# Local attention: queries and keys projected two groups ahead, transposed behind the half-array run; row 0's weights turned in blocks of 32 on VectorE

## The chip, the cores and the metric

The kernel runs on one core of one Trainium2 chip, in 32-bit floating point throughout. A core has five engines with a queue of their own each, which work in order and wait for one another through semaphores: TensorE (PE in the profile; its weight loads are shown apart as PEld), VectorE (DVE), ScalarE (ACT), GpSimd (POOL) and SyncE (SP), which here issues all DMAs. TensorE writes into eight banks of PSUM, from which VectorE and ScalarE copy ("evict") the results to SBUF. The metric is the time on the device in microseconds.

## What is computed

The input x has 2 sequences of 4096 tokens with 256 channels. A first layer (RWKV style) adds a recurrence over time to x. Then come two identical layers, each with local attention and a gated feed-forward part. Cut to what the change touches, one such layer is:

```python
h = shift_token(x)                       # half of the channels one token later
q, k, v = split(h @ wqkv, 3)             # 8 heads of 64
q = l2norm(q) * q_scale ; k = l2norm(k) * k_scale
q, k = rotary_xpos(q, k)                 # q*cos*scale + rotate_half(q)*sin*scale
# windows of 128 tokens: each query sees itself and the 128 tokens before it
attn = softmax(where(mask, -big, q @ k.T), -1)
x = x + (attn @ v) @ wo
h = layernorm(shift_token(x)) ; a, g = split(h @ w1 + b1, 2)
x = x + (a * gelu(g)) @ w2 + b2
```

The mask leaves a query at place i of its window the places above or at i of the window before (packs and backs in the kernel are the two triangles) and the places up to i of its own.

## The kernel before

**Groups and rows.** The attention layers run over 128 groups of 128 tokens (NN = 128; a block is four groups, and there are 32 blocks: 2 sequences x 2 layers x 8). The loop `for n in range(NN + 2)` (L1469) goes over the groups; its pass n is called row n here. In row n stand, among others, the scores, softmax and transposed weights of group n, the values and the output of group n - 1, q, k and v of group n + 1, and pieces of the feed-forward part of earlier blocks (fill). The recurrence of the second sequence is spread over some 50 rows of the first; the recurrence of the first sequence comes before the loop.

**Who sets the order.** The statements do not run in the order written. `Plan.note` records every operation with the row it belongs to (`plan.at`), its dependencies, and a cost from `Plan.cost` (L302). `Plan.order` (L376) then plays the engines forward: each time the engine that can start soonest takes, of the operations that can start at that time, the one of the lowest row and place. It knows how the eight banks come free, the shared lock of VectorE and GpSimd, the landing of DMAs, and a cost `TURN` when TensorE changes between its full array and a half of it. Operations marked `either` go to ScalarE or VectorE as they come free. `give` emits the result, so each engine's queue is fixed when the kernel is built, and every instruction has one line, L524 (L520 and L518 for scalings).

**The half-array run.** In `scores` (L1086) TensorE multiplies keys and queries of 64 rows each (`row` half), two heads side by side; in the same uninterrupted piece, `down_ends` comes ahead in some rows and `values(n - 1)` (L1183) follows, whose matmuls have 64 columns (`col` half): weights of the own window (pT with v) and of the window before (pB with dv, the difference of neighbouring v, made by GpSimd from a shifted copy vr). So one stretch per row runs on half arrays, and is entered from and left to full matmuls.

**q and k.** `project(n, j)` (L989) makes q (j = 0), k (1) or v (2) of group n: two matmuls of 128x512 into a bank, and a copy. `square` (ScalarE), `norms` (VectorE sum, then a power on GpSimd for the inverse root), `rotate` (GpSimd), `cosines` and `rotated` (VectorE) make the normalised, rotated q and k in place in `qk` (two buffers). `transpose_qk(n)` (L1062) turns them by eight TensorE transposes through two banks into qT and into one of three places of kT; on every second group a DMA copies one place of kT to another. It stands at the top of row n, ahead of the scores of group n.

**Row 0 of pB.** `transpose_p(n, s)` (L1157) turns the softmax weights of four heads at a time; ScalarE or VectorE copies them to pT, and VectorE multiplies them by the mask backs into pB. Row 0 of pB is different: it is the first column of pr, the weight of the oldest place. At s = 1 a ninth transpose, of 128x8, turns that column for all eight heads; a copy takes its 8 rows from PSUM to `last`, and one DMA writes them into row 0 of pB. The matmuls of values(n) that read pB wait for that DMA.

Of the kernel before, what the change touches and what calls it, by code (L numbers as in the profile page):

```python
# [15 lines left out]
P = 128  # L16
B, S, D = 2, 4096, 256
HD_A = 16
L, HEADS, DH, W = 2, 8, 64, 128
# [42 lines left out]
SLACK = 1.06  # L62
LOAD = 1283
LAND = 2500
TURN = {"row": 195, "col": 95, "full": 199}
SETS = {AF.Exp: 1, AF.Tanh: 1, AF.Gelu: 2, AF.Ln: 3}
QUADS = 4

# [112 lines left out]
class Plan:  # L181
# [194 lines left out]
    def order(self):  # L376
# [49 lines left out]
        while todo:  # L426
            for e in engines:
                if e not in stale:
                    continue
                best = None  # L430
                cands = []
                for t, g in waiting[e]:
                    s = earliest(e, t, g)
                    if e == "vector" and g[0].eng == "either" and free["scalar"] < max(t, free[e]) + LEAN:
                        continue
                    if s is not None:
                        cands.append((max(s, free[e]), g))
                if not cands:
                    pick[e] = None
                    continue  # L440
                t0 = min(s for s, _ in cands)
                for s, g in cands:
                    if s <= t0 + 1:
                        key = g[0].at
                        if best is None or key < best[0]:
                            best = (key, s, g)
                pick[e] = (best[1], best[2])
            stale = set()
            e = min((e for e in engines if pick[e]), key=lambda e: pick[e][0], default=None)
            assert e is not None, "no operation can start"  # L450
            t, g = pick[e]
            for o in g:
                if e == "tensor" and o.half != half:
                    t += TURN[o.half]
                    half = o.half
                if e == "scalar" and o.set not in (None, table):
                    t += LOAD
                    table = o.set
                for p in o.banks:
                    b = min((i for i in range(8) if banks[i] is not None), key=lambda i: banks[i])  # L460
                    p.bank, banks[b] = b, None
                    p.real = self.bank_tiles[b]
                    counts[p] = (len(p.users), 0.0)
                step, time = o.step, o.time
                if o.eng == "either" and e == "vector":
                    n = o.outs[0].idx.size
                    time = 150 + 1.04 * n if o.name == "copy" else 155 + 0.98 * n
                    step = time - 85
                    o.lock, o.hold = o.name == "scaled", time
                if o.eng == "either":  # L470
                    o.eng = e
                if e not in ("tensor", "sync"):
                    step, time = step * SLACK, time * SLACK
                o.start = t
                if e == "sync":
                    dma = max(dma, t) + o.passes
                    o.end = max(t + time, dma + LAND)
                else:
                    o.end = t + time
                if o.lock and e in lock:  # L480
                    lock[e] = t + o.hold
                t += step
                done.append(o)
                for p in o.uses:
                    c, last = counts[p]
                    counts[p] = (c - 1, max(last, o.end))
                    if c == 1:
                        banks[p.bank] = counts[p][1]
                        stale.add("tensor")
            free[e] = t  # L490
            if g[0].lock:
                stale.update(lock)
            stale.update(("vector", "scalar") if e == "scalar" else (e,))
            for x in engines:
                n = len(waiting[x])
                waiting[x] = [c for c in waiting[x] if c[1] is not g]
                if len(waiting[x]) != n:
                    stale.add(x)
            for nxt in after.get(id(g), ()):
                left[id(nxt)] -= 1  # L500
                if not left[id(nxt)]:
                    ready(nxt)
                    stale.update(("scalar", "vector") if nxt[0].eng == "either" else (nxt[0].eng,))
            todo -= 1
# [23 lines left out]
def kernel(ctx: ExitStack, tc: tile.TileContext, a: dict, out: bass.AP):  # L528
# [329 lines left out]
    w2 = tile_of([P, NM, D], "w2")  # L858

    def weights(l, which):  # L860
        if "qkv" in which:
            for j in range(3):
                cols = slice(j * INNER, (j + 1) * INNER)
                nc.sync.dma_start(out=wqkv[:, :, cols], in_=a["w_qkv"][l][:, :, cols])
        if "o" in which:
# [244 lines left out]
    def softmax(n, g):  # L1110
# [42 lines left out]
        for m in range(2):  # L1153
            ph = prs[n][:, h0 + 2 * m, off:]
            nc.either.scaled(ph, ph, sums[:, m : m + 1])

    def transpose_p(n, s):  # L1157


# [14 lines left out]
            ALU.mult,  # L1174
        )
        if s:
            pt = bank([P, W])
            nc.tensor.transpose(pt[:HEADS, :], pr[:, :, 0], ident)
            last = tile_of([P, W], "last", 2)[:HEADS]
            either(last, pt[:HEADS, :])  # L1180
            nc.sync.dma_start(out=pBs[n][0:1], in_=last)

    def values(n):  # L1183

# [268 lines left out]
    rec2.start()  # L1453
    plan.at(-1)
    nc.gpsimd.memset(ends, 1.0)
    load(0)
    mixed_out(0)
    transpose_x(0)
    load(1)
    table(0)  # L1460
    for j in range(3):
        project(0, j)
    square(0)
    rotate(0, 0)
    rotate(0, 1)
    norms(0)
    cosines(0)
    rotated(0)
    for n in range(NN + 2):  # L1469
        k, w = divmod(n, NW)  # L1470
        here, ahead, behind = n < NN, n + 1 < NN, 0 < n <= NN
        plan.at(n)
        if here:
            transpose_qk(n)
        for c in range(rec2.n):
            if NW + 1 + int(c * R_SLOTS / rec2.n) == n:
                plan.at(n + 0.5)
# [7 lines left out]
        plan.at(n)  # L1485

        first, l = ahead and (n + 1) % (NB * NW) == 0, ((n + 1) // (NB * NW)) % L
        if w == 3 and k + 2 < NK:
            load(k + 2)
        if w == 0 and k + 1 < NK:  # L1490
            mixed_out(k + 1)
        if 1 < n < NN + 2:
            normed(hs[(n - 2) // NW][:, (n - 2) % NW, :])
        if ahead:
            table(n + 1)
            if first:
                weights(l, "qkv")
            project(n + 1, 0)
            rotate(n + 1, 0)
        if here:  # L1500
            scores(n)
            differences(n)
        else:
            with piece():
                if n == NN:
# [4 lines left out]
        if here:  # L1510
            softmax(n, 0)
            softmax(n, 1)
        if ahead:
            project(n + 1, 1)
            square(n + 1)
            rotate(n + 1, 1)
        if behind:
            output(n - 1)
            shift(n - 1)
# [1 line left out]
                weights(n // (NB * NW) % L, "o")  # L1521
        if w == 1 and 0 < k < NK:
            transpose_h(k - 1)
        if w == 2 and k + 1 < NK:
            transpose_x(k + 1)
        if here:
            softmax(n, 2)
            softmax(n, 3)
        if ahead:
            norms(n + 1)  # L1530
        fill(n, 0)
        if here:
            transpose_p(n, 0)
        if ahead:
            project(n + 1, 2)
            cosines(n + 1)
        fill(n, 1)
        if here:
            transpose_p(n, 1)
        if ahead:  # L1540
            rotated(n + 1)
        fill(n, 2)
        fill(n, 3)
        if w < 2 and NW < n < NN and (n - NW - w) % (NB * NW) == 0:
# [83 lines left out]
```

## Time and profile before

| | |
|---|---|
| median of 3 runs | 2966.02 us (2964.07 to 2966.45) |
| the profiled execution | 2965.18 us, its span from first to last instruction 2963.4 us |
| TensorE busy | 2942.4 us, 99% of the span |
| VectorE, ScalarE, GpSimd busy | 76%, 68%, 49% |
| granted TensorE clock | 1.0 in all slices |
| transposes of row 0 on TensorE | 124 |
| copies to last | 97 on ScalarE, 250 ns; 27 on VectorE, 269 ns (medians) |
| DMAs pB<-last | 124, 693 ns each on SyncE's queue (median) |

A group of the profile is named by the tiles it writes and reads: `bank<-mats,pr` are transposes of softmax weights (mats holds the identity), `bank<-mats,qk` those of q and k, `bank<-wqkv,xT` the projections, `bank<-kT,qT` the scores, `bank<-pT,vt` and `bank<-pB,dv` the values, `bank<-hT,w` and `bank<-w,hm` the feed-forward part, `bank<-wo,oT` the output. `128*64` after it are the rows and columns of the array that are used. A 32-bit matmul is recorded as two instructions, a transpose as one. Matmuls overlap in the array, so the durations of a group add up to more than the time it takes; the distance between starts tells that time.

### The profile page before, as it was taken

How to read it: one execution, taken by the hardware profiler on the slowest of the kernel's cores; microseconds unless marked ns; L12 is line 12 of the kernel's file. 1: busy time of each engine (PE TensorE's matmuls, PEld its weight loads, DVE VectorE, ACT ScalarE, POOL GpSimd, SP SyncE). 2: the span in 40 equal slices, each digit the busy share in tenths (PEclk: the TensorE clock that was granted, in tenths of full speed). 3: DMA queues.
4: the chain of work that ended last, by engine and by line, in shares of the span. 5: the costliest groups of instructions: out<-in, count | busy, mean ns of one | idle time of the engine just before them, and what ended most of it. 6: DMA issues, size and time to landing. Idle time of an engine off the chain costs nothing.

```text
span 2963.4 us, 49081 instructions
## 1 busy us (share of the span) xinstructions
PE 2942.4 (99%) x15592; PEld 1919.1 (65%) x15592; DVE 2253.5 (76%) x5095; ACT 2023.8 (68%) x5377; POOL 1449.2 (49%) x1705
## 2 busy tenths in 40 slices
PE   9999999999999999999999999999999999999999
PEld 4476766666666666666666666666666666666667
DVE  7889999998866788786777667777776676767674
ACT  7887787778666777776666666665666666666664
POOL 2226654555554555445555444444554554555550
PEclk9999999999999999999999999999999999999999
DMA  2324322221121211111122221121112211111110
GB/s 85 114 78 135 113 69 88 74 81 54 60 65 54 79 49 54 59 57 56 54 71 84 75 66 50 58 62 58 58 41 71 70 58 51 56 53 54 49 42 28
DMA packets 185228, 195.10 MB, mean 66 GB/s; under 512 B 27812, under 2 KB 148484, under 8 KB 184456
## 3 DMA queue, kind: packets, MB, share of 16 engines
q1 hardware_dynamic: 184968, 191.96, 21.1%
q8 instruction: 123, 2.02, 0.3%
q14 instruction: 137, 1.12, 0.1%
HBM read 85.46 MB, written 39.85 MB: 42 GB/s over the span
## 4 chain that ended last, share of the span: by engine, by line
PE 90%; DVE 5%; ACT 4%; issue 1%; DMA 0%; POOL 0%; ACTq 0%; DVEq 0%; POOLq 0%
PE bank L524 90%; ACT pr L524 1%; ACT L524 1%; DVE arena L524 1%; DVE sq L524 1%; DVE bank L524 1%; ACT pr L520 1%; DVE hm L524 0%; DVE nmx L524 0%; DVE qk L524 0%; DVE x L524 0%; DVE pB L524 0%; DVE rn L524 0%; ACT hm L524 0%; ACT arena L524 0%
## 5 line engine op out<-in xcount | busy, mean ns | idle before, releaser
L524 PE MATMUL bank<-wqkv,xT 128*128 128x512 f32 x1536 | 723.8, 596 | 0.5 <-ACT xT L524 0.5
L524 PE MATMUL bank<-hT,w 128*128 128x512 f32 (+2 forms) x1452 | 651.7, 582 | 0.4 <-ACT hT L524 0.4
L524 POOL TENSOR_TENSOR t<-qk,tab 128x256 f32<-128x256 f32 x512 | 385.0, 772 | 467.9 <-ACT qk L524 360.5
L524 ACT ACTIVATE pr<-bank,nmx 128x129 f32<-128x129 f32 (+1 forms) x1024 | 370.6, 381 | 149.2 <-DVE nmx L524 147.9
L524 PEld LDWEIGHTS bank<-hT,w 128*128 128x128 f32 (+1 forms) x1452 | 262.7, 188 | 252.9 <-issue 237.7
L524 PEld LDWEIGHTS bank<-wqkv,xT 128*128 128x128 f32 x1536 | 266.4, 191 | 210.9 <-issue 207.5
L524 POOL TENSOR_TENSOR rn<-rn,mhalf 128x16 f32<-128x16 f32 x128 | 391.7, 3060 | 8.7
L520 ACT ACTIVATE pr<-pr,sums 128x129 f32<-128x129 f32 (+1 forms) x948 | 334.1, 419 | 40.5 <-DVE pr L524 40.1
L524 DVE COPY_PREDICATED bank<-packs,bank 128x254 f32<-128x254 int32 x496 | 186.4, 420 | 228.5 <-PE bank L524 228.3
L524 PE MATMUL bank<-w,hm 128*128 128x256 f32 x1280 | 294.2, 381 | 0.0
L524 POOL TENSOR_TENSOR dv<-vr,vt 128x512 f32<-128x512 f32 x124 | 164.6, 1327 | 200.2 <-PE bank L524 187.2
L524 PEld LDWEIGHTS bank<-w,hm 128*128 128x128 f32 x1280 | 239.7, 190 | 35.0 <-issue 4.2
L524 ACT COPY qk<-bank 128x512 f32<-128x512 f32 x225 | 132.6, 589 | 170.6 <-PE bank L524 164.1
L524 PE MATMUL bank<-kT,qT 64*128 64x256 f32 (+1 forms) x2048 | 246.1, 380 | 0.4 <-ACT kT L524 0.4
L524 PE MATMUL bank<-wo,oT 128*128 128x256 f32 x1024 | 243.3, 380 | 2.2 <-ACT oT L524 2.0
L524 PEld LDWEIGHTS bank<-wo,oT 128*128 128x128 f32 x1024 | 193.3, 190 | 71.9 <-ACT oT L524 24.2
L524 PEld LDWEIGHTS bank<-kT,qT 64*128 64x128 f32 x2048 | 190.4, 187 | 68.8 <-issue 35.2
L524 DVE TENSOR_TENSOR pB<-bank,backs 128x512 f32<-128x512 f32 x248 | 170.2, 686 | 82.6 <-PE bank L524 56.1
L524 ACT COPY hm<-bank 128x512 f32<-128x512 f32 (+1 forms) x175 | 100.8, 576 | 178.3 <-PE bank L524 177.3
L524 ACT ACTIVATION_READ_ACCUMULATOR pr<-bank,nmx 128x1 f32 x1024 | 222.3, 217 | 0.0
L524 PEld LDWEIGHTS bank<-mats,pr 128*128 128x128 f32 x1148 | 134.5, 135 | 115.9 <-issue 73.0
L524 PE MATMUL bank<-pT,vt 128*64 128x128 f32 x2048 | 203.3, 279 | 0.0
(159 smaller groups left out, 5628.8 us busy)
## 6 DMA issues: line engine op xcount, KB each, us to landing
vr<-vt SPq DMA_DIRECT2D x124, 224.0 KB
tab<-in_c_rot_dram SPq DMA_DIRECT2D x128, 128.0 KB
kT<-kT SPq DMA_DIRECT2D x64, 256.0 KB
z<-zd SPq DMA_DIRECT2D x16, 512.0 KB
x<-in_x_dram SPq DMA_DIRECT2D x16, 512.0 KB
x1d<-x SPq DMA_DIRECT2D x16, 512.0 KB
x<-x1d SPq DMA_DIRECT2D x16, 512.0 KB
h<-x SPq DMA_DIRECT2D x128, 64.0 KB
```

The source lines that it names most:

```text
L520: self.nc.scalar.activation(dst, src, AF.Copy, scale=scale)
L524: getattr(getattr(self.nc, o.eng), name)(*args, **kw)
```

## The change

Four things are changed together.

1. q and k of group n + 2, no longer of n + 1, are projected, normalised and rotated in row n; those of groups 0 and 1 come before the loop. v stays one group ahead. The weights of a new layer are loaded for q and k in the row that first projects with them, those for v one row later; `transpose_x` moves from the third row of a block to the second.
2. `transpose_qk(n + 1)` is noted in row n behind the scores of group n, no longer at the top of its own row. The transposes of group 0 come before the loop.
3. In `Plan.order`, when TensorE stands on a half array, transposes that can start within 150 ns of the earliest candidate are taken ahead of all else, and leaving the half array by a transpose is charged 150 ns (full matmul: 199). The charges for entering the row and the column half are exchanged (95 and 195).
4. Row 0 of pB: the ninth transpose, its bank and its copy go. GpSimd copies the 128x8 column of weights into a square of 128x32 (two buffers, cleared once), VectorE transposes it in blocks of 32x32, and four DMAs write the first eight rows of each block of 32 partitions to row 0 of pB, 32 places each.

```diff
@@ -62,7 +62,7 @@
 SLACK = 1.06
 LOAD = 1283
 LAND = 2500
-TURN = {"row": 195, "col": 95, "full": 199}
+TURN = {"row": 95, "col": 195, "full": 199, "turn": 150}
 SETS = {AF.Exp: 1, AF.Tanh: 1, AF.Gelu: 2, AF.Ln: 3}
 QUADS = 4
 
@@ -439,7 +439,13 @@
                     pick[e] = None
                     continue
                 t0 = min(s for s, _ in cands)
-                for s, g in cands:
+
+                turns = [] if e != "tensor" or half == "full" else [
+                    c for c in cands if c[0] <= t0 + TURN["turn"] and c[1][0].name == "transpose"
+                ]
+                if turns:
+                    t0 = max(s for s, _ in turns)
+                for s, g in turns or cands:
                     if s <= t0 + 1:
                         key = g[0].at
                         if best is None or key < best[0]:
@@ -451,7 +457,7 @@
             t, g = pick[e]
             for o in g:
                 if e == "tensor" and o.half != half:
-                    t += TURN[o.half]
+                    t += TURN["turn" if o.name == "transpose" else o.half]
                     half = o.half
                 if e == "scalar" and o.set not in (None, table):
                     t += LOAD
@@ -858,8 +864,8 @@
     w2 = tile_of([P, NM, D], "w2")
 
     def weights(l, which):
-        if "qkv" in which:
-            for j in range(3):
+        for j, t in enumerate("qkv"):
+            if t in which:
                 cols = slice(j * INNER, (j + 1) * INNER)
                 nc.sync.dma_start(out=wqkv[:, :, cols], in_=a["w_qkv"][l][:, :, cols])
         if "o" in which:
@@ -1154,6 +1160,8 @@
             ph = prs[n][:, h0 + 2 * m, off:]
             nc.either.scaled(ph, ph, sums[:, m : m + 1])
 
+    squares = [tile_of([P, 32], f"square{i}") for i in range(2)]
+
     def transpose_p(n, s):
 
 
@@ -1174,11 +1182,12 @@
             ALU.mult,
         )
         if s:
-            pt = bank([P, W])
-            nc.tensor.transpose(pt[:HEADS, :], pr[:, :, 0], ident)
-            last = tile_of([P, W], "last", 2)[:HEADS]
-            either(last, pt[:HEADS, :])
-            nc.sync.dma_start(out=pBs[n][0:1], in_=last)
+
+            q, t = squares[n % 2], tile_of([P, 32], "turned", 2)
+            nc.gpsimd.tensor_copy(q[:, :HEADS], pr[:, :, 0])
+            nc.vector.transpose(t, q)
+            for i in range(0, W, 32):
+                nc.sync.dma_start(out=pBs[n][0:1, :, i : i + 32], in_=t[i : i + HEADS, :])
 
     def values(n):
 
@@ -1453,25 +1462,33 @@
     rec2.start()
     plan.at(-1)
     nc.gpsimd.memset(ends, 1.0)
+    for t in squares:
+        nc.gpsimd.memset(t, 0.0)
     load(0)
     mixed_out(0)
     transpose_x(0)
     load(1)
     table(0)
-    for j in range(3):
-        project(0, j)
-    square(0)
-    rotate(0, 0)
-    rotate(0, 1)
-    norms(0)
-    cosines(0)
-    rotated(0)
+    project(0, 2)
+    for n in range(2):
+        if n:
+            plan.at(0)
+            table(n)
+        for j in range(2):
+            project(n, j)
+        square(n)
+        rotate(n, 0)
+        rotate(n, 1)
+        norms(n)
+        cosines(n)
+        rotated(n)
+        if n == 0:
+            transpose_qk(0)
     for n in range(NN + 2):
         k, w = divmod(n, NW)
         here, ahead, behind = n < NN, n + 1 < NN, 0 < n <= NN
         plan.at(n)
-        if here:
-            transpose_qk(n)
+        next2 = n + 2 < NN
         for c in range(rec2.n):
             if NW + 1 + int(c * R_SLOTS / rec2.n) == n:
                 plan.at(n + 0.5)
@@ -1485,21 +1502,24 @@
         plan.at(n)
 
         first, l = ahead and (n + 1) % (NB * NW) == 0, ((n + 1) // (NB * NW)) % L
+        first2, l2 = next2 and (n + 2) % (NB * NW) == 0, ((n + 2) // (NB * NW)) % L
         if w == 3 and k + 2 < NK:
             load(k + 2)
         if w == 0 and k + 1 < NK:
             mixed_out(k + 1)
         if 1 < n < NN + 2:
             normed(hs[(n - 2) // NW][:, (n - 2) % NW, :])
-        if ahead:
-            table(n + 1)
-            if first:
-                weights(l, "qkv")
-            project(n + 1, 0)
-            rotate(n + 1, 0)
+        if next2:
+            table(n + 2)
+            if first2:
+                weights(l2, "qk")
+            project(n + 2, 0)
+            rotate(n + 2, 0)
         if here:
             scores(n)
             differences(n)
+            if ahead:
+                transpose_qk(n + 1)
         else:
             with piece():
                 if n == NN:
@@ -1510,10 +1530,10 @@
         if here:
             softmax(n, 0)
             softmax(n, 1)
-        if ahead:
-            project(n + 1, 1)
-            square(n + 1)
-            rotate(n + 1, 1)
+        if next2:
+            project(n + 2, 1)
+            square(n + 2)
+            rotate(n + 2, 1)
         if behind:
             output(n - 1)
             shift(n - 1)
@@ -1521,24 +1541,27 @@
                 weights(n // (NB * NW) % L, "o")
         if w == 1 and 0 < k < NK:
             transpose_h(k - 1)
-        if w == 2 and k + 1 < NK:
+        if w == 1 and k + 1 < NK:
             transpose_x(k + 1)
         if here:
             softmax(n, 2)
             softmax(n, 3)
-        if ahead:
-            norms(n + 1)
+        if next2:
+            norms(n + 2)
         fill(n, 0)
         if here:
             transpose_p(n, 0)
         if ahead:
+            if first:
+                weights(l, "v")
             project(n + 1, 2)
-            cosines(n + 1)
+        if next2:
+            cosines(n + 2)
         fill(n, 1)
         if here:
             transpose_p(n, 1)
-        if ahead:
-            rotated(n + 1)
+        if next2:
+            rotated(n + 2)
         fill(n, 2)
         fill(n, 3)
         if w < 2 and NW < n < NN and (n - NW - w) % (NB * NW) == 0:
```

## The prediction

> **What bounds the kernel now.** I read the page's first part, then the chain of waits, then the busy time by stretch, then TensorE's own timeline in the steady part. First the page, the chain and the stretches (after the times: TensorE busy, weight loads, VectorE, ScalarE, GpSimd, each with its count; clock; DMA share; GB/s):
>
> ```profile
> span 2963.4 us, 49081 instructions
> PE 2942.4 (99%) x15592; PEld 1919.1 (65%) x15592; DVE 2253.5 (76%) x5095; ACT 2023.8 (68%) x5377; POOL 1449.2 (49%) x1705
> ...
> PE 90%; DVE 5%; ACT 4%; issue 1%; DMA 0%; POOL 0%; ACTq 0%; DVEq 0%; POOLq 0%
> ...
> 0.00:200.00 200.00, 191.12 (x569) 102.37 (x570) 164.41 (x311) 161.02 (x274) 51.61 (x101) 1.00 0.26 89
> 200.00:300.00 100.00, 95.36 (x486) 67.99 (x486) 89.80 (x216) 70.73 (x173) 58.30 (x77) 1.00 0.40 134
> 300.00:1000.00 700.00, 698.18 (x3836) 461.11 (x3834) 598.28 (x1356) 519.61 (x1384) 368.75 (x446) 1.00 0.24 73
> 1000.00:2000.00 1000.00, 998.79 (x5460) 658.49 (x5457) 747.40 (x1713) 672.20 (x1845) 509.06 (x581) 1.00 0.20 62
> 2000.00:2900.00 900.00, 899.14 (x4936) 582.96 (x4935) 630.50 (x1443) 574.93 (x1635) 455.63 (x491) 1.00 0.18 55
> ```
>
> TensorE is the bound. From 300 to 2900 us it lacks 1.82 + 1.21 + 0.86 = 3.9 us in 2600; the other 17 idle us lie in the ramp-up (8.9 and 4.6) and the tail. So what TensorE issues decides, and its mean durations mislead: matmuls overlap, and what one costs is the distance from its start to the next start. The timeline gives that (start, duration of the group, operation):
>
> ```profile
> 1566.20 0.39 PE L524 MATMUL bank<-pB,dv 128*64 128x128 f32 x4
> 1566.52 1.09 PE L524 MATMUL bank<-mats,x 128*128 128x128 f32 x8
> 1567.45 1.88 PE L524 MATMUL bank<-hT,w 128*128 128x512 f32 x4
> 1569.17 1.89 PE L524 MATMUL bank<-wo,oT 128*128 128x256 f32 x8
> 1570.90 1.88 PE L524 MATMUL bank<-hT,w 128*106 128x512 f32 x4
> 1572.61 0.60 PE L524 MATMUL bank<-mats,pr 128*128 128x128 f32 x4
> 1573.05 1.88 PE L524 MATMUL bank<-wqkv,xT 128*128 128x512 f32 x4
> 1574.77 0.71 PE L524 MATMUL bank<-mats,pr 128*128 128x128 f32 x5
> 1575.32 1.88 PE L524 MATMUL bank<-wqkv,xT 128*128 128x512 f32 x4
> 1577.03 3.60 PE L524 MATMUL bank<-hT,w 128*128 128x512 f32 x8
> 1580.47 1.04 PE L524 MATMUL bank<-mats,qk 128*128 128x128 f32 x8
> 1581.34 1.88 PE L524 MATMUL bank<-wqkv,xT 128*128 128x512 f32 x4
> ...
> 1586.66 0.39 PE L524 MATMUL bank<-pB,dv 128*64 128x128 f32 x4
> 1586.98 1.98 PE L524 MATMUL bank<-hT,w 128*128 128x512 f32 x4
> 1588.80 1.46 PE L524 MATMUL bank<-wo,oT 128*128 128x256 f32 x6
> ```
>
> To be seen: four transposes take 0.44 us (1572.61 to 1573.05), five take 0.55 (1574.77 to 1575.32); the fifth is row 0's. Four 512-wide instructions take 1.72 us (1573.05 to 1574.77), but 1.82 directly behind the half-array run (1586.98 to 1588.80): +0.10. Eight transposes take 0.87 us (1580.47 to 1581.34), and 0.93 behind the run (1566.52 to 1567.45): +0.06. The step out of the run itself (last group of pB to the next start) is 0.32 either way.
>
> **What the Trainium skill says.** "TensorEngine Tiling (Array Packing)", Key Properties: a change of tiling mode drains TensorE. The trace agrees: full instructions ahead of each other leave no gap, while each run pays about 0.1 us at each change. "DMA: Bandwidth & Descriptors", Anatomy of one DMA: some 2.0 us fixed per DMA, most of it the receipt of the write. The trace shows only ends: 0.69 us for SyncE to issue row 0's DMA, and the earliest use of its data 3.2 us after that issue began. "VectorE: DVE Perf Modes", The three transpose paths: VectorE transposes 32x32 blocks only, 311 ns for 128x128 bf16. No row of the kernel before shows it.
>
> **The change, part by part.**
>
> *A. Row 0 off TensorE.* 124 transposes (128x8) go: 124 x 0.109 (0.87 / 8) = 13.5 us, all on the bound. In the instruction order nothing else leaves TensorE: every other kind keeps its count, and the run is entered and left as often (127 times from its column half).
>
> *B. Transposes behind the run.* Before, of 127 runs 23 are followed by transposes and 104 by wide matmuls; after, 114 and 13 (95 of them q/k's, often only one of the two groups of four). So 91 runs change their follower, worth 0.10 - 0.06, I take 0.045: 4.1 us (3.6 to 4.6 from the rounding).
>
> *C. Q and k two groups ahead.* Moves, adds nothing to TensorE. Group 1's projections come before the first scores, inside the ramp-up stretch; x's transposes come one row (some 20 us) sooner after mixed_out, whose chain behind its matmuls (VectorE add, statistics, four powers of 0.6 us, scale) is an estimated 8 us. Weights of a new layer are still asked for in the row that first uses them. I take 0, with -3 to +3 us for a reshuffled ramp-up.
>
> *D. Row 0's new path.* Gone: 97 ScalarE copies of 0.25 us and 27 VectorE copies of 0.27. Added per row: a GpSimd copy of 128x8 (no such row; xT's 128x1 copy is 0.19, arena's 128x2 is 0.46: I take 0.3), a VectorE transpose of 128x32 (between the 0.15 us of the small operations and the page's 0.31: 0.2), and four DMAs for one, so 372 more issues. Together 37 us on GpSimd (49% busy), 25 on VectorE against 7 saved, 372 x 0.69 = 257 us on SyncE's queue, which spends about 916 us of the span issuing. All lie beside TensorE, so they cost nothing unless late.
>
> The added waits: VectorE's transpose waits for the GpSimd copy, which in 78 of 124 rows stands right behind the 3.06 us power of q/k's norms; behind the transpose VectorE has rotated's product, a q/k eviction, or pB. The four DMAs wait at the head of SyncE's queue, with kT's copy or the next vr behind them. TensorE waits for the last of them at the first pB matmul. Chain after the last pr transpose: 0.31 us to pB's start when VectorE is free, up to 1.0 at the median; 0.69 for pB; 0.06 to the first DMA; three issues of about 0.7 (2.1); the last DMA, 2.0 by the page (at most 3.2 by the trace). Sum 5.2 to 5.9, bounds 5.2 to 7.1. The cover is TensorE's work between that transpose and the first pB matmul, from the new instruction order with the distances above: median 7.7 us, at least 6.4 in all but two rows, with 20 rows at 6.4 to 6.5. So there are 0.5 to 1.2 us to spare and I cost it at 0. Summed over the rows, a chain of 6.5 would cost 4 us, 7.0 costs 15, 7.5 costs 32, 8.0 costs 64.
>
> *Sum.* 13.5 + 4.1 = 17.6 us. The profiled execution took 2965.18 (span 2963.4 and 1.8 around it), giving 2947.6; the median of the runs lies 0.8 higher: **2948**.
>
> What is late next: nothing but TensorE again, 99% busy; softmax keeps its distance to its transposes (at least 7.3 us of TensorE work behind the scores in the steady part of the new order, 5.2 before).
>
> **The rivals.**
>
> *1. More than the sum.* With q/k ready early, TensorE has work in the ramp-up's holes: of the 13.5 us idle before 300 us, 8 vanish. 2940. For: 4.6 us idle in 200 to 300, where attention starts. Against: most of the first 8.9 is the first load and the recurrence's chain, which q/k can't fill.
>
> *2. Partly given back.* Just after the run four banks hold scores, one the values, up to two down_ends' sums. A q/k transpose takes a bank for only 0.44 us of TensorE work where a projection gave 0.86, so evictions must keep up: 0.06 us lost on each of 127 rows eats 8 us. 2956. For: VectorE and ScalarE are busiest there (2.0 and 1.46 us of the 2 us from 1520.5). Against: each takes 0.59 us an eviction and they share them.
>
> *3. Slower: row 0's DMAs come last.* One mechanism: four issues one after another, behind GpSimd and other traffic on SyncE, hold the first pB matmul. At a chain of 7.1 us it eats the 17.6 us, at 7.4 the kernel is slower by over 0.2%; at 7.5 it is 2948 + 32 = 2980. For: SyncE's queue often waits at its head (vr's DMAs 654 us in total), and a large weight transfer may lie ahead. Against: 7.1 needs the trace's longest landing and a late VectorE in every row.
>
> That the change doesn't do what it says is in B already: 13 runs still end in wide matmuls.
>
> **How the numbers follow.** No change means within 0.2%, some 6 us, about what a measurement of this kernel can tell. Forecast 0.68 (2943 to 2953), rival 1 0.11, rival 2 0.12 (a third of it above 2960), rival 3 0.09 (0.01 of it within 0.2%). Faster 0.68 + 0.11 + 0.08 = 0.87; same 0.04 + 0.01 = 0.05; slower 0.08. The range takes rival 1 and rival 2's upper end and leaves rival 3 out: 2938 to 2962.
>
> **What would show it.** A right: no 128*8 group on TensorE, groups of five become four. B right: groups behind pB mostly mats,qk, 0.04 us less per run. C right: q/k projections unchanged in number and still without idle time. D right: almost no idle time at pB,dv; SyncE's new DMAs 0.7 us apart. Wrong: TensorE's busy share below 99% from 300 to 2900 us, with waits on the DMA pB<-turned (rival 3) or on evictions to banks (rival 2).

## The result, and the profile after

The changed kernel takes 2971.4 us (median of 12 runs, 2969.4 to 2975.3), the kernel before 2966.1 us (12 runs, 2964.1 to 2966.6): a ratio of 1.0020 with an interval of 1.0012 to 1.0029. It is slower by 0.2%, where 2948 us, a gain of 0.6%, was predicted. The profiled execution took 2975.2 us; its span is 2973.4 us, 10.0 us more than before.

The page of the changed kernel, first part and chain of waits:

```profile
span 2973.4 us, 49246 instructions
PE 2934.7 (99%) x15468; PEld 1918.0 (65%) x15468; DVE 2256.7 (76%) x5228; ACT 1990.7 (67%) x5242; POOL 1490.6 (50%) x1831
...
PE 87%; DVE 7%; ACT 5%; issue 1%; DMA 0%; SPq 0%; POOL 0%; DVEq 0%; ACTq 0%
```

TensorE has its 124 instructions less (15592 before), and is still the bound. But its share of the chain fell from 90% to 87%, and VectorE's and ScalarE's rose by 2 and 1 points. A point is 30 us here, so this gives a direction and no size. Where the time went, the stretches say (TensorE busy, weight loads, VectorE, ScalarE, GpSimd; then the clock):

```profile
200.00:300.00 100.00, 90.63 (x414) 63.49 (x414) 82.94 (x196) 65.90 (x142) 53.64 (x70) 0.93 0.38 124
300.00:1000.00 700.00, 691.28 (x3776) 457.13 (x3774) 603.39 (x1392) 507.18 (x1347) 383.12 (x484) 1.00 0.24 73
1000.00:2000.00 1000.00, 997.61 (x5468) 660.63 (x5466) 757.62 (x1780) 653.29 (x1780) 524.93 (x629) 1.00 0.21 63
2000.00:2900.00 900.00, 897.60 (x4927) 585.03 (x4922) 621.66 (x1487) 573.53 (x1624) 471.28 (x533) 1.00 0.19 55
```

From 200 to 300 us TensorE does 414 instructions where it did 486, is idle for 9.4 us instead of 4.6, and has a mean clock of 0.93 instead of 1.00 (two times 6.8 us at half clock). From 300 to 1000 us it idles 8.7 instead of 1.8. So 11.6 of the 17.7 us of added idle time lie ahead of 1000 us, and a part of the loss isn't idle time at all: busy time counts an instruction at half clock as fully busy.

The busy share misleads again, so I made the same sum as in the prediction over the whole run of TensorE: each distance from a start to the next, less what that instruction takes back to back at full clock in the trace (0.429 us for 512 columns, 0.2155 for 256, 0.109 for 128, half of it on a half array), less what a change of half takes (0.096 us into the row half, 0.196 from row to column half, 0.148 out, and 0.104 or 0.056 on the next instruction if it is wide or a transpose). What is left over is waiting and slow clock:

| us, from TensorE's first to its last instruction | before | after | difference |
|---|---|---|---|
| the instructions | 2849.3 | 2835.8 | -13.5 |
| changes of half | 68.9 | 64.5 | -4.4 |
| what is left over | 35.7 | 62.9 | +27.2 |
| sum | 2953.9 | 2963.2 | +9.3 |

Both savings came as predicted (13.5 and 4.1). 27.2 us more than before were lost elsewhere. The largest waits of TensorE name most of it (us in total, times, longest):

```profile
PE bank L530 <- DVE qk L530: 10.3, 7, 3.7
PE bank L530 <- ACT arena L530: 7.8, 6, 6.1
PE bank L530 <- DVE hm L530: 2.7, 4, 1.6
PE bank L530 <- ACT oT L530: 2.2, 5, 0.8
PE bank L530 <- DVE ends L530: 2.2, 1, 2.2
PE bank L530 <- DVE xT L530: 2.2, 5, 1.3
PE bank L530 <- POOL x L530: 2.0, 1, 2.0
```

The waits for arena (the recurrence) and hm are there before too, with 7.8 and 2.3 us. The one for qk was 0.8 us: now 10.3. The waits for DVE ends (2.2), DVE xT (2.2) and "POOL x" (2.0, read below) are not in the list of before.

**One hole and what follows it.** TensorE's timeline around the second of the large waits, called holes from here on (start, duration of the group, operation, and in brackets the idle time before it):

```profile
281.09 3.60 PE L530 MATMUL bank<-wqkv,xT 128*128 128x512 f32 x8
284.52 1.89 PE L530 MATMUL bank<-wot,z 128*128 128x256 f32 x8
289.58 1.94 PE L530 MATMUL bank<-mats,qk 128*128 128x128 f32 x8 [3.16 <-DVE qk L530]
291.31 5.73 PE L530 MATMUL bank<-wqkv,xT 128*128 128x512 f32 x8
296.97 1.35 PE L530 MATMUL bank<-kT,qT 64*128 64x256 f32 x10
```

Eight transposes took 0.87 us from start to start in the prediction's lines; here it is 1.73 (289.58 to 291.31). The same group of eight wide instructions takes 3.60 at 281.09 and 5.73 at 291.31. The records of the granted clock say 0.5 from 288.8 us on, for 6.8 us, so to 295.6. So this hole costs 3.3 us of waiting and then half of the 6.0 us from 289.58 on.

In this profile there are five such places: 3.8 us of waiting at 252 us, 3.3 at 286, 1.9 and 1.4 close together at 531, 2.2 at 2388, 2.3 at 2945 (counted from start to start; the brackets show some 0.1 to 0.2 us less), and with them come 6.8, 6.8, 3.4, 3.4 and 3.4 us at half clock, 22 us of these behind the hole's end. That is 14.9 us of waiting and 11 us (half of 22) of slow clock, together 25.9 us; the 27.2 are net of the one hole that the kernel before has alone, 2.4 us at 252 us, and small waits make up the rest. In the profiled execution of the kernel before no record says half clock between 12 us (ahead of that both kernels start at half rate: transposes 0.21 us apart, later 0.109) and the end of TensorE's work. Its other executions were not all free of it: in 15 of the 26 beside e1 to e4 the mean clock was 0.999, and these took 1.0 us longer on average than those at 1.000.

**Why q and k come late.** VectorE's timeline ahead of 289.58, and GpSimd's line that belongs to it:

```profile
280.42 0.69 DVE L530 TENSOR_TENSOR x<-x,bank 128x512 f32<-128x512 f32 x1 [1.69 <-PE bank L530]
281.02 1.21 DVE L530 TENSOR_REDUCE rn<-sq 128x16 f32<-128x1024 f32 x1
...
284.19 1.23 DVE L530 TENSOR_TENSOR sq<-sq,t 128x1024 f32<-128x1024 f32 x1
285.33 0.42 DVE L530 BATCH_NORM_STATS2 st<-x 128x6 f32<-128x256 f32 x1
285.67 0.73 DVE L530 TENSOR_TENSOR_SCAN arena<-arena,s 128x256 f32<-128x256 f32 x1
286.45 0.69 DVE L530 TENSOR_TENSOR x<-x,bank 128x512 f32<-128x512 f32 x1
...
287.74 1.70 DVE L530 TENSOR_TENSOR qk<-sq,rn 128x1024 f32<-128x1024 f32 x1
```

```profile
282.67 2.94 POOL L530 TENSOR_TENSOR rn<-rn,mhalf 128x16 f32<-128x16 f32 x1
```

There is no bracket from 280.42 on: VectorE works without a pause. The sum of the norms goes out at 282.2, GpSimd gives the inverse roots back at 285.6, and the last product qk<-sq,rn starts only at 287.74, 2.1 us later, behind a scan of the recurrence, an addition to x, statistics and row 0's new transpose. These 2.1 us are the larger part of the hole of 3.3. The hole at 252 us looks the same: the inverse roots are ready at 252.25, and the product starts 2.2 us later, behind the first scores' row maxima.

```profile
249.32 2.93 POOL L530 TENSOR_TENSOR rn<-rn,mhalf 128x16 f32<-128x16 f32 x1
254.42 1.22 DVE L530 TENSOR_TENSOR qk<-sq,rn 128x1024 f32<-128x1024 f32 x1
255.70 1.97 PE L530 MATMUL bank<-mats,qk 128*128 128x128 f32 x8 [3.65 <-DVE qk L530]
```

In both places VectorE's queue, not TensorE, sets the time.

**Row 0's DMAs, once.** SyncE's queue and then TensorE's timeline around 2388 us:

```profile
2383.70 0.88 SPq L530 DMA_DIRECT2D vr<-vt  x1
2384.63 0.84 SPq L530 DMA_DIRECT2D h<-x  x1
2385.52 0.56 SPq L530 DMA_DIRECT2D vr<-vt  x1
2386.18 2.70 SPq L530 DMA_DIRECT2D pB<-turned  x4
```

```profile
2387.66 0.44 PE L530 MATMUL bank<-pT,vt 128*64 128x128 f32 x4
2390.09 0.44 PE L530 MATMUL bank<-pB,dv 128*64 128x128 f32 x4 [1.98 <-POOL x L530]
```

VectorE had finished pB at 2384.6, but an h and a vr transfer stand ahead of the four in the queue. The last of the four is issued at about 2388.2, and pB is first used 1.9 us later. "DMA: Bandwidth & Descriptors", Anatomy of one DMA, in the Trainium skill gives some 2.0 us fixed, for DMAs that GpSimd issues; the prediction took this figure for SyncE's without saying so, and this row agrees. The wait's named releaser, GpSimd's x, is not the cause (in e10 below, with the same wait shortened, the DMA itself is named). In the other rows no wait on these four is among the large ones.

**Transposes behind the run.** A steady row:

```profile
1579.78 0.39 PE L530 MATMUL bank<-pB,dv 128*64 128x128 f32 x4
1580.10 1.09 PE L530 MATMUL bank<-mats,qk 128*128 128x128 f32 x8
1581.03 1.88 PE L530 MATMUL bank<-wqkv,xT 128*128 128x512 f32 x4
1582.75 1.89 PE L530 MATMUL bank<-wo,oT 128*128 128x256 f32 x8
```

0.93 us for the eight transposes and 1.72 for the four wide ones, as the prediction read it; nothing waits there.

### The profile page after: what moved, and what is told of

The parts are those of the page before. It is cut to its first block, busy times and chain, and to the rows that moved or that the text cites. A ratio compares the mean times of both kernels' runs of the same rounds, so it can differ in the third digit from the quotient of the medians.

```text
span 2973.4 us, 49246 instructions
## 1 busy us (share of the span) xinstructions
PE 2934.7 (99%) x15468; PEld 1918.0 (65%) x15468; DVE 2256.7 (76%) x5228; ACT 1990.7 (67%) x5242; POOL 1490.6 (50%) x1831
## 4 chain that ended last, share of the span: by engine, by line
PE 87%; DVE 7%; ACT 5%; issue 1%; DMA 0%; SPq 0%; POOL 0%; DVEq 0%; ACTq 0%
PE bank L530 87%; DVE arena L530 1%; DVE sq L530 1%; ACT pr L530 1%; ACT L530 1%; DVE hm L530 1%; ACT arena L530 1%; DVE pB L530 1%; DVE qk L530 1%; DVE bank L530 1%; ACT pr L526 1%; DVE nmx L530 0%; DVE rn L530 0%; DVE x L530 0%; ACT hm L530 0%
## 5 line engine op out<-in xcount | busy, mean ns | idle before, releaser
L530 PE MATMUL bank<-hT,w 128*128 128x512 f32 (+3 forms) x1452 | 645.7, 580 | 0.2 <-ACT hT L530 0.2
L526 ACT ACTIVATE pr<-pr,sums 128x129 f32<-128x129 f32 (+1 forms) x919 | 326.9, 421 | 33.2 <-DVE pr L530 32.8
L530 ACT COPY qk<-bank 128x512 f32<-128x512 f32 x212 | 126.5, 597 | 209.2 <-PE bank L530 185.2
L530 PEld LDWEIGHTS bank<-mats,pr 128*128 128x128 f32 x1024 | 128.1, 141 | 121.1 <-issue 80.4
```

The lines of the kernel that those rows point to most:

```text
L526: self.nc.scalar.activation(dst, src, AF.Copy, scale=scale)
L530: getattr(getattr(self.nc, o.eng), name)(*args, **kw)
```

## The experiments

Each kernel ran several times beside the kernel before, whose median was 2965.2 us in e1 to e4, 2966.3 in e5 to e8, 2965.9 in e9 to e11 and 2965.4 in e12. The first four expectations name as T1 the theory that the savings are real and the lookahead loses where it starts, in the ramp-up; their other theories put the loss on row 0's new path or on the steady part.

**e1_row0_only.** The kernel before with row 0's new path alone.

```diff
-            nc.tensor.transpose(pt[:HEADS, :], pr[:, :, 0], ident)
...
-            nc.sync.dma_start(out=pBs[n][0:1], in_=last)
+            nc.gpsimd.tensor_copy(q[:, :HEADS], pr[:, :, 0])
+            nc.vector.transpose(t, q)
+            for i in range(0, W, 32):
+                nc.sync.dma_start(out=pBs[n][0:1, :, i : i + 32], in_=t[i : i + HEADS, :])
```

> The kernel before with the new path of row 0 alone (GpSimd copy, VectorE transpose, four DMAs); q and k one group ahead, the planner's charges as before. Theory 1 (the gain of 13.5 us on TensorE is real, and the lookahead loses it in the ramp-up): 2966.1 - 13.5 = 2952.6 us, up to 4 us more if the DMAs of row 0 come late once as they do at 2390 us after the change. Theory 2 (row 0's new path holds TensorE all along the run): 2966 us or more.

Measured: 2953.6 us, ratio 0.9960 (0.9948 to 0.9973). Step A is right: 12 us less. D's wait at pB is hidden too: none is in the trace. But what is left over rises by 5.0 us (40.7 against 35.7). Some 4 of these lie in the tail, where a hole of 2.3 us is new and 6.8 us at half clock follow it. The other window of 6.8 us, at the old hole at 252 us, costs less than 1 us net: most of the 3 us that TensorE loses to the clock there it waits less afterwards.

**e2_ahead_only.** The changed kernel with row 0's old path (the diff of e1 undone).

> The changed kernel with row 0's path as before (ninth transpose on TensorE, one copy, one DMA). Theory 1: the three holes of TensorE in the ramp-up stay (10 us idle and 8 us at half the clock), against 4 us gained behind the half-array runs: 2978 to 2985 us. Theory 2: without row 0's new path what is left is the gain behind the runs: 2962 us.

Measured: 2967.7 us, ratio 1.0007 (0.9999 to 1.0015). Neither number: the lookahead and the followers together bring nothing, or a loss of up to 0.15%. Its changes of half take 64.2 us, 4.7 less than before, and what is left over is 42.3, with holes of 3.8 us at 255 and 3.6 at 302 and 6.8 us at half clock behind each. That e1's gain of 11.6 and e2's loss of 2.5 don't add up to the changed kernel's loss of 5.3 shows that the parts meet: the holes at 531 and 2388 us of the changed kernel are in neither of the two.

**e3_turns_only.** The kernel before with the order's preference and charges alone.

```diff
-TURN = {"row": 195, "col": 95, "full": 199}
+TURN = {"row": 95, "col": 195, "full": 199, "turn": 150}
...
+                turns = [] if e != "tensor" or half == "full" else [
+                    c for c in cands if c[0] <= t0 + TURN["turn"] and c[1][0].name == "transpose"
+                ]
```

> The kernel before with the planner's part of the change alone: transposes preferred behind a half-array run, and the exchanged charges. q and k are one group ahead, so only transposes that are ready then can follow a run. Theory 1: no holes, a gain of 0 to 4 us: 2962 to 2966 us. Theory 3 (it is the preference that disturbs the order and opens the holes): 2975 us or more.

Measured: 2966.8 us, ratio 1.0004 (0.9996 to 1.0013), about no change. 83 runs have transposes behind them (23 before), which saves 2.8 us of changes; what is left over rises by 4.5 us, by 3.4 us at half clock behind the hole at 252 us and by waits of about 1 us at new places.

**e4_late20.** The whole change, but one group ahead until row 20 and two from there on.

```diff
+        m = n + 1 if n < S_AHEAD else n + 2
...
-            project(n + 2, 0)
+            project(m, 0)
```

> The whole change, but q and k go two groups ahead only from row 20 on (group 21 is made in addition in row 19); the ramp-up runs as before. Theory 1: the three holes of the ramp-up and their half clock, some 19 us, are gone: 2950 to 2955 us. Theory 4 (two groups ahead cost in every row, by banks or by VectorE and GpSimd): 108 of 128 rows still pay, so 2968 us or more.

Measured: 2957.4 us, ratio 0.9971 (0.9960 to 0.9982), above T1's range but far from T4's: 14 us of the loss hang on the first 20 rows. It stays 3.8 us above e1, although changes of half take some 3 us less. One hole of 2.3 us at pB, at 2373 us, and 3.4 us at half clock behind it make 4.0 of this difference of some 7; waits of 0.6 to 1.5 us that e1 doesn't have make up the rest.

**e5_after_fill.** Now the price of the half clock. In the changed kernel, TensorE gets 217 transposes of the identity into a free bank where the kernel's own order leaves it idle.

```diff
+            idle = t - free["tensor"]
+            if e == "tensor" and half == "full" and idle > FILL and free["tensor"] > 0:
...
+                    while u + 2 * 110 < t:
...
+                        o.eng, o.name, o.start, o.end, o.n = "tensor", "transpose", u, u + 110, -1
```

> The changed kernel with some 210 transposes of the identity, into a bank that is free then, put where the kernel's own order leaves TensorE without work for more than 0.6 us: some 34 at 252 us, 32 at 283, 10 to 15 at 437, 519 and 2360, 24 near the end, a few between the recurrence's steps. The results of these transposes are not used, all else is as changed. T5 (the five holes cost twice: some 15 us of waiting, and 11.9 us because TensorE runs at half clock for 3.4 or 6.8 us behind each of them): the waits stay, the clock records behind them are gone or down to one, so 2971.4 - 11.9, about 2959.5 us (2957 to 2964). Rival R (the clock records go with the holes but what is lost there is the waiting alone): 2969 to 2973.

Measured: 2970.7 us, ratio 1.0015 (1.0009 to 1.0022). The half clock is gone in all 21 runs (mean clock 1.000), and the time isn't: that is rival R's number. But the comparison is spoiled by the edit itself. Matched to the changed kernel matmul by matmul, this one is 1.7 us later at 180 us, where transposes stand between the recurrence's steps, and from 1554 to 2385 us it loses 1.8 us of its lead of 2.2 again, most of it to its own 15 transposes ahead of the run there (which gets back what it waited at pB). So e5 doesn't decide.

**e6_row0_turns.** e1 and e3 together, no lookahead.

> Row 0's weights on VectorE and the order's preference for transposes behind the half-array run, without the lookahead of two groups. T1 (the run's cheaper follower is worth some 0.05 us each, and e3 showed none of it because new holes with half clock ate it): e1's 2953.6 less 60 x 0.05 = 3 us, 2950 to 2952. Rival R (the follower is worth nothing): 2953 to 2955. In both the holes at 251 us and near the end stay.

Measured: 2954.1 us, ratio 0.9957 (0.9945 to 0.9970), as e1 within the interval. 80 runs have a transpose behind them. The saving of 1.8 us of changes against e1 is in the trace, but too small to be told in the time.

**e7_row0_turns_fill** and **e8_late20_fill.** The same transposes as in e5, in e6 and in e4.

> e6_row0_turns with the identity transposes in the holes (23 at 250 us, 24 near the end, a few between the recurrence's steps). T5: half clock of 3.4 to 6.8 us at each of the two holes is gone, half of that is saved: 3 to 6 us less than e6, 2945 to 2948. Rival R (only the waiting costs): as e6, within 1 us.

> e4_late20 with the identity transposes in its holes (250, 2351 and 2905 us the large ones). T5: three windows of 3.4 us at half clock go, 5 us: 2957.4 - 5 = 2952 (2950 to 2954). Rival R (only the waiting costs): 2956 to 2958.

Measured: 2954.0 us, ratio 0.9958 (0.9945 to 0.9970), and 2961.0 us, ratio 0.9982 (0.9974 to 0.9990). Clock 1.000 in every run, no gain in e7 and a loss of 3.5 us in e8: matched matmul by matmul, e8 is 2.0 us later than e4 at 181 us already, and 3.9 us at 1541 us. Filling small holes too cost at least what it brought.

**e9_after_fill_few.** The transposes only where the trace has a large hole, and ended earlier.

```diff
-FILL = 600
+FILL = 1500
...
-            if e == "tensor" and half == "full" and idle > FILL and free["tensor"] > 0:
+            if e == "tensor" and half == "full" and idle > FILL and free["tensor"] > 200000:
...
-                    while u + 2 * 110 < t:
+                    while u + 7 * 110 < t:
```

> e5_after_fill with the identity transposes only where the changed kernel's trace has one of its five large holes (29 at 252 us, 27 at 283, 10 at 519, 10 at 2360, 13 near the end), ended 0.8 us before the order's next real instruction; none between the recurrence's steps, where e5's cost 1.7 us, and none in the small holes. T5 (the half clock behind the holes costs half of its length, and e5 lost that gain again on its own transposes): no clock record below full speed, and the median falls to 2964 to 2967 us, which is where the changed kernel's own runs point when its mean clock (0.996: 2975.2; 0.997: 2972.4; 0.998: 2969.9) is carried on to 1.000. Rival R (the half clock costs nothing that shows in the time): 2969 to 2972.

Measured: 2966.3 us, ratio 1.0002 (0.9994 to 1.0010) against 1.0020 (1.0012 to 1.0029) of the changed kernel: 5 us come back although 89 useless instructions were added and the transposes of q and k start no sooner (at 255.77 and 289.56 us, 255.70 and 289.58 before). The place of the hole shown above:

```profile
284.59 1.89 PE L547 MATMUL bank<-wot,z 128*128 128x256 f32 x8
286.31 3.11 PE L534 MATMUL bank<-mats 128*128 128x128 f32 x27
289.56 1.09 PE L547 MATMUL bank<-mats,qk 128*128 128x128 f32 x8
290.49 3.60 PE L547 MATMUL bank<-wqkv,xT 128*128 128x512 f32 x8
294.02 2.00 PE L547 MATMUL bank<-kT,qT 64*128 64x256 f32 x16
```

The transposes of q and k start at 289.56 as they did (289.58), so no wait got shorter. But from there to the scores it takes 4.46 us instead of 7.39. That is the price of the half clock, measured by itself at one place: 2.9 us. One window of 3.4 us is left in this profile, behind two waits of 0.7 and 1.4 us at 273 to 275 us. Matched to the changed kernel's profile matmul by matmul, this kernel keeps the 2.9 us; the 2.8 us that the fill at 252 us brings are gone again by 281 us, in these two waits and that window. Over the whole profile it is 8.9 us ahead, of a changed kernel's run that was one of the slowest.

The changed kernel's own runs point the same way, though the seven at 0.997 alone lie up to 4.1 us apart. By the mean clock of the run: 0.996, 2975.2 us (one run); 0.997, 2972.4 (mean of seven); 0.998, 2969.9 (mean of four). Carried on to 1.000 that is about 2965.

**e10_late20_dmas_first.** e4 with row 0's DMAs preferred on SyncE's queue.

```diff
+                if e == "sync":
+                    turns = [
+                        c for c in cands if c[0] <= t0 + 1000 and any(v.place in urgent for v in c[1][0].ins)
+                    ]
```

> e4_late20 with one more preference in the order: of the transfers that SyncE can issue within 1 us, row 0's four go first, ahead of an h and a vr transfer that stood in front of them at the one large hole ahead of pB's first matmul (2.3 us and 3.4 us at half clock in e4). T6 (that hole is the whole of what the four transfers cost): the hole shrinks to 0.7 us, its half clock goes, 2957.4 - 1.5 - 1.7 = 2954 (2953 to 2956). Rival R6 (the transfers' place doesn't matter, what is lost against e1 lies in the steady part's small waits): 2956.5 to 2958.5.

Measured: 2956.6 us, ratio 0.9969 (0.9958 to 0.9980): the rival's number. But its trace has the hole as T6 had it:

```profile
2372.89 0.44 PE L536 MATMUL bank<-pT,vt 128*64 128x128 f32 x4
2373.81 0.44 PE L536 MATMUL bank<-pB,dv 128*64 128x128 f32 x4 [0.47 <-DMA pB<-turned]
```

From pT to the first pB it takes 0.92 us, 0.27 in a steady row: 0.7 us of waiting instead of 2.3, now with the DMA named as releaser, and no half clock behind it. From row 21 to the tail what is left over falls from 17.4 us to 13.8. In the ramp-up it rises from 10.9 to 13.6: the preference changed the order of other work too, and three waits of 1.1 to 1.8 us are new at 283, 515 and 601 us. The mechanism at pB is shown; that mending it would pay without such a side effect is not.

**e11_row0_turns_fill_few.** e6 with transposes in its two large holes alone, the version of all these that looked best.

> e6_row0_turns with the identity transposes in its two large holes alone (18 at 250 us, 13 near the end), ended 0.8 us before the next real instruction. T5: two windows at half clock (3.4 and 6.8 us in e6's profile, mean clock of its runs 0.998 to 0.999) go, 2 to 5 us less than e6's 2954.1: 2949.5 to 2952. Rival R (nothing gained by the clock): 2953 to 2955.

Measured: 2951.7 us (2951.2 to 2952.3), ratio 0.9954 (0.9941 to 0.9966), the fastest kernel of the study. Its stretches:

```profile
200.00:300.00 100.00, 97.20 (x510) 69.30 (x510) 88.80 (x218) 70.44 (x173) 57.67 (x80) 1.00 0.38 125
300.00:1000.00 700.00, 697.43 (x3804) 462.39 (x3801) 594.30 (x1389) 526.67 (x1373) 382.69 (x480) 1.00 0.25 75
1000.00:2000.00 1000.00, 999.09 (x5472) 656.53 (x5471) 745.49 (x1759) 666.60 (x1812) 530.80 (x630) 1.00 0.20 61
```

The clock is 1.00 throughout, and 3.5 us are idle from 300 to 2000 us (11.1 in the changed kernel). Matched to e6's profile matmul by matmul, all of the gain, 3.0 us, comes from the fill near the end. The 1.3 us that the fill at 250 us brings by 258 us are gone by 272 us, in waits for q and k, oT and softmax. So half clock costs its full price only where TensorE is what the others wait for behind it.

**e12_late4.** e4's edit with the start in row 4.

```diff
-S_AHEAD = 20
+S_AHEAD = 4
```

> The whole change, but the lookahead goes from one group to two only in row 4 (e4_late20: in row 20), so that the first scores again have only group 0's projections ahead of them. T7 (the ramp-up's loss lies in the first four rows, where group 1's projections stand ahead of the first scores and VectorE has three groups' norms to do beside the recurrence): the holes of 3.8, 3.3, 1.8 and 1.0 us between 250 and 315 us go, the one of 2.4 us of the kernel before comes back, and two windows of 6.8 us at half clock become one of 3.4 to 6.8: 7.5 + 4 less than the changed kernel's 2971.4, 2958 to 2962. Rival R7 (the loss moves with the row in which the lookahead starts, or lies in rows 4 to 20, where x's transposes come a row sooner): 2964 or more.

Measured: 2958.1 us, ratio 0.9978 (0.9970 to 0.9986), in T7's range. Only the first four rows and what stands ahead of them differ in the program from the changed kernel, and 13 us are back. Not all of them lie in these rows, because the order behind them shifts too: in the two profiles what is left over is some 10 us less from 200 to 350 us, 4.5 less from 350 to 650, and some 4 less behind 2370 us, where the hole at pB is 1.4 us and the tail's hole comes without half clock. TensorE's timeline there:

```profile
252.01 3.80 PE L531 MATMUL bank<-hm,wold 128*128 128x256 f32 x8 [2.16 <-DVE hm L531]
255.60 1.06 PE L531 MATMUL bank<-mats,pr 128*128 128x128 f32 x4
256.45 1.06 PE L531 MATMUL bank<-mats,arena 128*128 128x128 f32 x4
257.30 2.31 PE L531 MATMUL bank<-wot,z 128*128 128x256 f32 x8
259.45 1.04 PE L531 MATMUL bank<-mats,qk 128*128 128x128 f32 x8
```

The first scores have one group's projections ahead of them again, the hole of the kernel before at 252 us is back (here with 6.8 us at half clock behind it), and q and k are in time.

## Why the prediction was wrong, step by step

**A (13.5 us) was right.** 13.5 us of instructions went, and e1, where nothing else is changed, gained 11.6.

**B (4.1 us) was right in size, and no run shows it in the time.** Changes of half take 4.4 us less; 114 runs have transposes behind them, as counted. But in e3 and e6 the order that gets this saving makes new waits of about 1 us, or a difference too small to see.

**C is the step that failed.** "I take 0, with -3 to +3 us for a reshuffled ramp-up." It cost some 13 us, with what follows from it further on: e12 gives them back by changing four rows. The prediction looked at what C adds to TensorE, found nothing, and stopped. In the ramp-up VectorE is nearly as full as TensorE: the prediction's own line for 200 to 300 us has it busy for 89.80 of 100 us. C puts VectorE's share of group 1's norms and rotation into that stretch ahead of the first scores, so VectorE gives q and k back late; the two holes at 252 and 286 us both wait for DVE qk. The bound I had named is a mean over the span, and I used it in a stretch where another engine is nearly as full. That VectorE is the cause is read from the timeline: no run took work off VectorE alone; e12 shows that the loss hangs on the early start. The holes could have been seen beforehand: the order that the kernel computes when it is built has them, since e5's edit, which looks at that order alone, put 34 transposes into the hole at 252 us and 32 into that at 286, some 3.7 and 3.5 us of work. The prediction took from this order who follows the runs, and not where it leaves TensorE idle. That x's transposes come one row sooner is not shown to cost anything: the wait for xT at 533 us is 1.3 us, but it follows one for q and k, and in e12, where they come sooner from row 4 on, no wait for xT is over 0.4 us.

**The term that was missing is the clock.** The prediction priced a stall as its own length. Behind 17 of 19 holes of 2.2 us or more TensorE ran at half clock for 3.4 or 6.8 us; in the changed kernel this is worth 5 us of the median (e9), and up to 11 in the profiled run, one of the slowest. "TensorE: Matmul & The Clock Gate", Part 1, in the Trainium skill states the mechanism: a free-running window of 3.4 us, half clock after an idle window; how the traces agree is told at the end. I had looked only at the clock of the kernel before, which was 1.0 everywhere, and didn't ask what a new hole would do to it. Holes and clock together, 25.9 us in that run, outweigh the 17.9 us saved.

**D, costed at 0, held in e1's steady rows and failed in one place of the whole change, and perhaps in the tail.** Rival 3's mechanism, DMAs queued behind other transfers so that pB comes last, is what happens at 2388 us, but in one row and not in every one: 2.2 us and 1.7 of slow clock. So rival 3's 2980 us is not what made the kernel slower.

**Rival 1 had the ramp-up the wrong way round.** It was to fill holes there; it made them. Rival 2 (evictions too slow behind the run) isn't seen: TensorE's wait for oT, the largest for an eviction behind the run, is 2.2 us in all, 2.0 before.

What stays open is the tail's hole of 2.3 us (a wait for VectorE's ends; before, the largest wait near the end is 0.6 us): it comes with row 0's path in e1 and e6, in e4, e10 and e12, and with the whole change, and not in e2 and e3. In e1 it and its half clock make some 4 us, so the new path may not be free even alone. A table load of 1.28 us and the activations of hm and ends stand ahead of it on ScalarE; why the order comes out so was not traced.

## What to carry to other kernels

Look for the bound in each stretch before moving work across stretches: an engine that is second over the whole span can be first where the work lands, and moving work "to where it is ready sooner" moves it in front of what is needed first. If the order is computed ahead, ask it where it leaves the bound idle. On TensorE price a wait of over 2 us at its length plus some 1.5 to 3 us for the clock, where TensorE is the bound behind it, and if the wait can't be removed, fill it with a few useless transposes that end before the real work. Filling smaller ones as well gained nothing here. When several edits come together, run each alone: here the edit worth 12 us was hidden by another's loss.

## What the runs showed of the hardware

**A hole halves the clock, and a grid of windows decides which.** In the profiles of all kernels, of 19 single holes of 2.2 us or more, 17 come with the record 0.5 for 3.4 or 6.8 us, starting between 1.4 us ahead of the hole's end and 1.8 us behind it. Two don't: the one near the end of e12, and the one at 252 us of the kernel before, though the same 2.39-us hole gave 3.4 us in e3, e4, e6 and e10 and 6.8 in e1 and e12. Holes of 1.2 to 1.9 us alone gave none (e4, e9, e10, e12); 1.9 and 1.4 us with 1.9 between their ends did, and 0.7 and 1.4 (e9).

The records say why. In every profile the half clock starts a whole number of times 3.413 us after the first record. Cut into such windows up to TensorE's end, the 14 profiles have 15 windows at full clock in which, by the profile, no matmul runs for 1.87 us or more: each of them is followed by half clock. Of six with 1.61 to 1.73 us four are, and of the other 11250, with 1.57 us or less, none. So in this case the border is near half a window. The tail's hole of e12 is cut by the grid into 1.18 and 1.05 us, and the kernel before has at most 1.46 us in a window. Why half clock lasts one window or two these figures don't tell. "TensorE: Matmul & The Clock Gate", HAM oscillation, in the Trainium skill warns of idle gaps over some 3.4 us; here 1.9 us within one window were enough.

**The clock goes with a part of the spread of a kernel's runs.** In the changed kernel 2.5 us lie between the means of the runs of mean clock 0.997 and of 0.998, where 0.001 of 2973 us is 3. But it isn't all: the runs of 0.997 lie up to 4.1 us apart, and with clock 1.000 in all runs e11's five lie within 1.1 us and e5's 21 within 3.0.

**Small prices that no row before had shown.** VectorE's transpose of 128x32 in 32-bit takes 0.20 us (194 to 214 ns, 124 of them in e1), and a DMA issue of 8 rows of 32 numbers 0.63 us in the median (496 of them in e1).
